# A two-layer graph-attention kernel: first steps with W1's loads and sums elsewhere and one scaling inside a sum; last group in another order, with its last norms applied on VectorE

## Chip, cores and metric

One core of a Trainium2 chip. The metric is the device time of one execution in microseconds (us), lower is better. The engines are TensorE (PE; PEld is its weight load), VectorE (DVE), ScalarE (ACT), GpSimd (POOL), and SyncE (SP), whose queue issues nearly all transfers here.

## What is computed

The input x holds 128 graphs of 128 nodes with 512 features in float32, adj holds a 128 x 128 adjacency matrix for each. Cut to what matters:

```python
# layer 0, 8 heads of 64
q, k, v = x @ Wq + bq, x @ Wk + bk, x @ Wv + bv
logits  = where(adj > 0, q k^T / sqrt(64), -1e9)          # per head
out     = softmax(logits) v                               # heads side by side
x       = layernorm(x + relu(out @ Wo + bo))
# layer 1, one head
Wh      = x @ W
e       = leaky((Wh @ a1)[:, None] + (Wh @ a2)[None, :])  # slope 0.2
att     = softmax(where(adj > 0, e, -9e15), over the first index)
x       = layernorm(x + leaky(att @ Wh))
```

## The kernel before

**Matrix products by seven.** Every product with a weight matrix is done by a Strassen scheme (Winograd's form): 7 block products in place of 8. The weight's side needs four block sums, made once (`right_blocks`, L149 to L156): t2 = t2 - t0, t5 = t3 - t2, t4 = t5 - t0, t6 = t1 - t5. The left side needs four sums for each group of graphs (`left_blocks`, L269 to L280, on GpSimd). The pieces of one product are named p1 to p7 (the block products on TensorE), t0, t2, t3 (copies of a bank by ScalarE between products that go into the same bank), and c11, c12, c21, c22 (result blocks, mostly by VectorE). p1 uses weight block 0, p5 block 2 (t2), p6 block 5, p2 block 1, p7 block 4, p4 block 6, p3 block 3 (`PLACE`, L147). p7 goes into p6's bank after t2 has been copied.

**Loop.** Graphs go in groups of 4. Q, K and V are made for a group at once (L366 matmuls, 128 x 256 results); pairs of graphs share the product with Wo (layer 0) and with W1 (layer 1) (L447). The loop runs over steps t = -3 to 123 (L974), one graph a step: scores (L518), mask and maxima on VectorE (L532, L541), exponentials and divisions on ScalarE (L552, L566), a store of the attention weights to DRAM (L573) and a fetch that re-reads them in blocks (L579), from which VectorE transposes (L583, paT), and a step later the product with V (L596, p_oT). `group()` takes the next step of the next group's Q, K and V, `pair()` the next of a pair's. V's weight blocks are kept in DRAM and fetched one by one into a ring of three buffers (wv_n, L407).

**First steps.** Wq's blocks 0 and 1 are scaled by 1/8 (L944), the first products start, and `other_half` (L959) takes graphs 2 and 3, then block 2: scaled, minus block 0; then `add_x`, the four left sums on GpSimd; then block 3: scaled, and the other three sums, on VectorE. In step 0 the loads of W1 are made into chores (L1006): two broadcasts of the vector a (256 KB each) and eight of W1 (128 KB each), of which each `group()` issues two. W1 gets an extra column W1 a: 8 `dots` of two VectorE instructions each (L205), four `last_column` of two (L220), then the four block sums; `w1_chores(4)` takes four of these 16, twice in step 3 (all dots) and twice in step 5.

**Order.** All five engines' queues have the order in which the code issues them (`manual_schedule`, L874): an engine takes its instructions in order, and a waiting one holds what is behind it.

**Last group.** The last four graphs' layer 0 and the last eleven graphs' layer 1 are written as one list, `PLAN` (L1231), of pieces name.method: v is the last group's V; s0 to s3 its softmaxes; sl, el, al what the loop left; a0 to a2 pairs of layer 0 (by, bw preload a bank with the bias); b0 to b4 pairs of layer 1; e0 to e10 the attention of layer 1 of graphs 117 to 127, x, m loads. An e runs sender (L794, ACT), turn (L798, PE transpose), add (ACT), maxima (DVE), exp (ACT), divide (DVE), product (L837, PE), copy (ACT), residual (L847, L848, DVE), stats (DVE), rstd (L646, L648, POOL), apply, store. With `on_scalar` (L649 to L660) rstd makes two more small GpSimd results (L651, L653), and the apply is a ScalarE instruction (L657); without it the apply is on VectorE (L661).

```python
1223    for n in range(11):
1224        jobs[f"e{n}"] = Edge(
...
1227            on_scalar=True,
```

Of the kernel before, what the change touches and what calls it, by code (L numbers as in the profile page):

```python
# [12 lines left out]
ALU = mybir.AluOpType  # L13
# [11 lines left out]
def kernel(  # L25
# [59 lines left out]
    nc = tc.nc  # L85
# [5 lines left out]
    QSCALE = 1.0 / float(HD) ** 0.5  # L91
# [54 lines left out]

    PLACE = (0, 1, 3, 6, 2, 5, 4)  # L147

    def right_blocks(t):  # L149

        return [
            lambda: nc.vector.tensor_sub(t[2], t[2], t[0]),
            lambda: nc.vector.tensor_sub(t[5], t[3], t[2]),
            lambda: nc.vector.tensor_sub(t[4], t[5], t[0]),
            lambda: nc.vector.tensor_sub(t[6], t[1], t[5]),
        ]  # L156

    def places(w):
        return [w[:, n] for n in range(7)]
# [30 lines left out]
    def load_w1():  # L190
# [7 lines left out]
        loads = [load_a(0), load_a(1)] + block_loads(W1, columns(w1), nc.sync)  # L198
# [30 lines left out]
        ops = [dots(k, o, c) for k, o in every for c in range(2)]  # L229
        return loads, ops + [last_column(k, o) for k, o in every] + right_blocks(places(w1))  # L230

    X, XT, XS, Q, K, V, MF, OT, X1T, X1, WH = ({} for _ in range(11))

# [662 lines left out]
    chores = []  # L896
# [46 lines left out]
    def scale(n):  # L943
        nc.vector.tensor_scalar_mul(wq[:, n], wq[:, n], QSCALE)  # L944

    wq_sums = right_blocks(places(wq))
    turned = [order_features(b) for b in range(2)]
    keep_busy(14)
# [10 lines left out]
    def other_half():  # L959

        for b in (2, 3):
            transpose_rows(b, order_features(b), nc.scalar.copy)
        scale(2)
        wq_sums[0]()
        add_x()
        scale(3)
        for op in wq_sums[1:]:
            op()

    chores += right_blocks(places(wk)) + load_wv()  # L970
    END = B - GROUP
# [2 lines left out]
    for t in range(-3, END):  # L974
# [17 lines left out]
        def w1_chores(n):  # L992
            for op in [w1_sums.pop(0) for _ in range(n)]:
                op()
# [7 lines left out]
        if t == 0:  # L1002
            load_blocks(Wo, columns(wo), nc.sync, spread_rows=False)
            late_chores = right_blocks(places(wo)) + load_bias()
            w1_loads, w1_sums = load_w1()
            chores += w1_loads  # L1006
        if t == 1:
            chores += late_chores

# [32 lines left out]
        elif t == 4:  # L1042
# [14 lines left out]
            layer.store(0)  # L1057
            layer.fetch(1)
            layer.fetch(0)
            sm.exp(6, 7)  # L1060
            group()
            sm.reciprocals(0)
# [3 lines left out]
        else:  # L1066
            sm.maxima()
            group()
            if t == 3:
                w1_chores(4)  # L1070
            if t == 5:
                turn_x1(4)
                x1_sums()
# [11 lines left out]
            pair()  # L1085
            sm.exp(0, 1, 2, 3)
            edge.exp()
            if t in (3, 5):
                w1_chores(4)
            pair()  # L1090
            sm.exp(4, 5)
            last.transpose()
# [130 lines left out]
    for n in range(11):  # L1223
        jobs[f"e{n}"] = Edge(
            END - 7 + n,
            {"z": z_homes[n % 4], "e": part(wk, 6, n % 4), "att": part(wk, 5, n % 4)},
            on_scalar=True,
        )
    for n in range(6):
        jobs[f"x{n}"] = jobs[f"m{n - 2}"] = Load(END - 2 + n)  # L1230
    PLAN = """  # L1231
        v.p5 x0.x el.residual m1.adj s0.scores m2.adj v.fetch al.apply.0 x1.x b0.p1
        sl.transpose al.fetch.1 v.p6 b0.t0 s0.add.0 m1.cast s0.add.1 m3.adj al.store.0
        s1.scores s0.reduce v.t2 v.fetch v.p2 m1.mask s0.exp.4.5 s1.add.0 s1.add.1 s0.exp.6.7
        al.fetch.0 s1.reduce b0.p6 s0.exp.0.1 b0.p5 s0.exp.2.3 v.c11 v.fetch s1.exp.4.5 v.p7
        s0.reciprocals.1 s0.reciprocals.0 el.stats s0.divide.2.3 al.transpose.1 s0.divide.4.5
        el.rstd b0.p2 b0.t2 al.transpose.0 s0.divide.0.1 b0.p7 al.sum.0 b0.c11 s0.divide.6.7
        b1.p1 al.sum.1 s1.exp.6.7 s0.store al.sum.2 b0.t3 s1.reciprocals.1 s1.exp.0.1 b0.p4
        b0.c22 al.sum.3 s1.divide.4.5 b0.p3 b0.c21 s0.fetch s1.divide.6.7 s2.scores b0.c12 v.t3
        e0.sender e0.turn s1.exp.2.3 v.c22 v.p4 m2.cast s1.reciprocals.0 e0.add m2.mask s2.add.0  # L1240
        s1.divide.2.3 v.p3 s2.add.1 s1.divide.0.1 b1.t0 s2.reduce s1.store v.c21 b1.p6 el.apply
        v.c12 s2.exp.2.3 el.store s3.scores e0.maxima s2.exp.6.7 s1.fetch sl.attend e0.exp
        s2.exp.4.5 e0.divide e1.sender e1.turn b1.p5 s0.transpose sl.copy e0.product m3.cast
        s2.reciprocals.1 sl.sum.0 e1.add m3.mask b1.p2 s3.add.0 s2.divide.6.7 sl.sum.1
        s1.transpose s2.divide.4.5 a0.by a0.p1 sl.sum.2 b1.t2 e0.copy sl.sum.3 b1.p7 b1.c11 a0.t0
        s3.add.1 s2.exp.0.1 a0.p6 s3.reduce b1.t3 s0.attend a0.t2 e0.residual s3.exp.0.1 a0.p7
        s3.exp.6.7 a0.bw a0.p5 b1.c22 x2.x a0.t3 s2.reciprocals.0 e1.maxima s3.exp.2.3 a0.p4
        s2.divide.0.1 a0.c22 b1.p3 e1.exp s3.reciprocals.0 s2.divide.2.3 a0.c21 a0.p3 e1.divide
        s3.divide.0.1 s2.store a0.stats.1 e1.product s3.divide.2.3 b1.c12 a0.rstd.1 s3.exp.4.5
        s1.attend e0.stats e1.copy e3.sender e3.turn s3.reciprocals.1 e0.rstd b1.p4 s0.copy e1.residual  # L1250
        s2.fetch s1.copy a0.p2 e1.stats x3.x s3.divide.6.7 a0.c11 s1.sum.0 a0.c12 s3.divide.4.5
        s1.sum.1 e3.add s3.store a0.stats.0 s1.sum.2 e0.apply a1.by a1.p1 b1.c21 e1.rstd e0.store
        e3.maxima a0.apply.1 e2.sender e2.turn a1.p2 a1.t0 a0.store.1 s2.transpose e3.exp a0.rstd.0 a1.p6
        e2.add s3.fetch e1.apply e2.maxima a1.bw a1.p5 s1.sum.3 a1.t2 a0.apply.0 e3.divide a1.p7
        e1.store e2.exp a1.c11 a0.fetch.1 s2.attend e2.divide a1.t3 a1.c22 a1.p4 s2.copy
        a0.store.0 s3.transpose a1.p3 a1.c21 a1.stats.1 s3.attend a0.transpose.1 a0.fetch.0
        a1.rstd.1 e3.product s3.copy a1.c12 e2.product e3.copy a1.stats.0 s3.sum.0 a2.p2
        a1.apply.1 s3.sum.1 e3.residual e2.copy a1.store.1 a2.bw a2.p5 s3.sum.2 a0.transpose.0 a2.by a2.p1
        a1.rstd.0 x5.x e2.residual b2.p1 a2.t0 a0.sum.0 a1.apply.0 a1.fetch.1 a2.p6 a2.c11
        s3.sum.3 b2.t0 e2.stats b2.p5 a0.sum.1 a2.t2 e3.stats x4.x a0.sum.2 a2.p7 a1.store.0  # L1260
        a0.sum.3 b2.p6 a2.t3 e2.rstd a2.c22 a2.p4 b2.t2 a1.transpose.1 a2.p3 e3.rstd e2.apply
        a1.fetch.0 a2.c21 b2.p7 a2.stats.1 e3.apply e4.sender e4.turn a2.c12 a2.rstd.1 b2.p2 e2.store
        b2.t3 e3.store e4.add b2.p4 a2.stats.0 a2.apply.1 b2.c22 a2.rstd.0 b2.c21 a2.store.1
        b2.c11 b2.p3 a1.transpose.0 e6.sender e6.turn e4.maxima a2.apply.0 a1.sum.0 b3.p1 e6.add
        a2.store.0 a1.sum.1 b2.c12 b3.p2 e4.exp e6.maxima b3.t0 a2.fetch.1 a1.sum.2 e5.sender e5.turn
        b3.p6 e4.divide a1.sum.3 e5.add e6.exp e5.maxima e4.product b3.t2 a2.fetch.0 e6.divide
        e5.exp b3.p7 b3.c11 e4.copy e5.divide e6.product b3.t3 e4.residual b3.p5 e6.copy
        e4.stats e5.product a2.transpose.0 e4.rstd b3.p4 e5.copy a2.transpose.1 b4.p2 b3.c22
        b3.c21 a2.sum.0 e4.apply e6.residual b4.p1 a2.sum.1 e4.store b3.p3 a2.sum.2 b4.t0
        e6.stats a2.sum.3 b4.p6 b3.c12 e6.rstd b4.c11 b4.p5 b4.t2 e5.residual b4.p7 e6.apply  # L1270
        e5.stats e8.sender e8.turn e6.store e7.sender e7.turn b4.t3 e8.add b4.p4 b4.c22 e5.rstd e7.add e8.maxima
# [50 lines left out]
```

## Time and profile before

| | us |
|---|---|
| median of 3 runs | 2402.37 (2400.96 to 2404.64) |
| the profiled execution | 2402.25 |
| its span, first to last instruction | 2400.4 |
| mean granted TensorE clock | 0.995 of full |
| PE busy | 2363.4 (98%) |
| PE waits listed, 0 to 100 us | 12.9 |
| PE waits listed, 175 to 2300 us | 1.2 |
| PE waits listed, 2300 to 2401 us | 11.8 |

The span is the time between the first and the last instruction of one execution. The list of waits names the engine and line that stood idle and what released it; a wait for several semaphores is put down to the one that came last by the profile, which can be the wrong one. A row of the timeline has start, duration, engine, line, operation, result and operands, shape, count, and in brackets the idle time before it. The table of stretches has, for each, the busy time and the clock that TensorE was granted, as a part of full speed.

### The profile page before, as it was taken

The page shows a single profiled execution, that of the slowest core. Times are in us where ns is not written, and L with a number is a line of the kernel's source. Part 1 is how long each engine was busy: PE and PEld are TensorE (multiplying, and loading weights), DVE is VectorE, ACT ScalarE, POOL GpSimd, SP SyncE. Part 2 cuts the span into 40 slices and gives each one's busy share as a digit, 9 for nine tenths or more (in the row PEclk, how much of TensorE's full clock was granted, in tenths as well). Part 3 has the DMA queues.
Part 4 walks back from the last instruction along what each step waited for, and adds up shares of the span by engine and source line. Part 5 has one row for each costly group of instructions (what it writes and reads, how often), then busy time and mean ns, then how long its engine had stood idle before and what let it go on. Part 6 is the DMA issues. An engine that isn't in the chain of part 4 may idle for free.

```text
span 2400.4 us, 44153 instructions
## 1 busy us (share of the span) xinstructions
PE 2363.4 (98%) x13362; PEld 1980.3 (82%) x13362; DVE 1827.0 (76%) x3719; ACT 1517.3 (63%) x5463; POOL 811.1 (34%) x1195
## 2 busy tenths in 40 slices
PE   8999999999999999999999999999999999999996
PEld 7888888888888888888888888888888888888874
DVE  5677787777777877877777778778778777777777
ACT  3666666566666666665666666666666666666685
POOL 1232333233333333332333433333323334333335
PEclk9999999999999999999999999999999999999999
DMA  7455555555546545555545555555554554554452
GB/s 205 158 165 160 174 163 162 176 161 158 179 147 186 164 154 174 160 165 181 159 154 183 154 176 167 156 173 157 169 181 157 157 179 155 173 175 151 156 170 98
DMA packets 435566, 395.32 MB, mean 165 GB/s; under 512 B 108280, under 2 KB 339328, under 8 KB 435328
## 3 DMA queue, kind: packets, MB, share of 16 engines
q1 hardware_dynamic: 435008, 392.23, 52.3%
q8 instruction: 107, 1.75, 0.3%
q14 instruction: 131, 1.07, 0.1%
q10 hardware_dynamic: 320, 0.26, 0.0%
HBM read 248.58 MB, written 143.72 MB: 163 GB/s over the span
## 4 chain that ended last, share of the span: by engine, by line
PE 91%; DVE 3%; DMA 2%; ACT 2%; issue 1%; SPq 1%; POOL 1%; DVEq 0%; ACTq 0%; POOLq 0%
PE st_y L366 27%; PE p_y L447 17%; PE st_w L366 13%; PE p_w L447 9%; PE st_x L366 7%; PE lg L518 6%; PE p_oT L596 5%; PE p_x L447 4%; PE p_h L837 4%; DMA wv_n<-wv 1%; ACT pa L552 0%; DMA x_dram<-x 0%; DMA wq<-in_L_gnn_Wq_dram 0%; ACT pa L566 0%; POOL rstd L648 0%
## 5 line engine op out<-in xcount | busy, mean ns | idle before, releaser
L552 ACT ACTIVATE pa<-pa,nmax 128x128 f32<-128x128 f32 x1008 | 392.6, 393 | 5.9 <-DVE nmax L541 5.5
L646 POOL TENSOR_SCALAR ve<-mv 128x1 f32<-128x1 f32 x256 | 69.9, 273 | 855.9 <-DVE mv L642 847.1
L566 ACT ACTIVATE pa<-pa,rs 128x128 f32<-128x128 f32 x1008 | 334.1, 395 | 8.6 <-DVE rs L562 8.5
L275 POOL TENSOR_TENSOR oS<-oT 128x256 f32<-128x256 f32 x63 | 45.8, 727 | 643.4 <-ACT oT L610 643.4
L532 DVE TENSOR_TENSOR pa<-lg,mf 128x512 f32<-128x512 f32 x252 | 161.9, 684 | 99.9 <-PE lg L518 99.6
L458 ACT COPY pr_t<-p_y 128x257 f32<-128x257 f32 (+1 forms) x375 | 137.7, 367 | 135.7 <-PE p_y L447 133.3
L343 ACT COPY st_t<-st_y 128x512 f32<-128x512 f32 x192 | 110.5, 575 | 144.2 <-PE st_y L366 143.1
L552 ACT ACTIVATION_READ_ACCUMULATOR pa<-pa,nmax 128x1 f32 x1008 | 192.3, 191 | 0.0
L347 ACT ACTIVATE st_t<-st_y,b_cols 128x256 f32<-128x256 f32 x192 | 80.6, 471 | 164.9 <-PE st_y L366 164.9
L648 POOL TENSOR_TENSOR rstd<-ve,mhalf 128x1 f32<-128x1 f32 x256 | 177.0, 691 | 21.4
L596 PEld LDWEIGHTS p_oT<-paT,v 128*64 128x64 f32 x2016 | 107.5, 136 | 91.8 <-PE st_y L366 44.0
L610 ACT ACTIVATE oT<-p_oT,b_cols 128x128 f32<-128x128 f32 x504 | 144.2, 368 | 60.0 <-PE p_oT L596 58.9
L583 DVE STREAM_TRANSPOSE paT<-paz 128x1024 f32<-128x1024 f32 x126 | 156.9, 1245 | 3.3 <-DMA paz<-pa_dram 2.1
L541 DVE TENSOR_REDUCE nmax<-pa 128x8 f32<-128x1024 f32 x126 | 153.7, 1220 | 4.4
L518 PE MATMUL lg<-kT,qT 64*128 64x128 f32 x2048 | 148.7, 285 | 0.0
L518 PEld LDWEIGHTS lg<-kT,qT 64*128 64x128 f32 x2048 | 124.2, 187 | 22.9 <-issue 22.9
L596 PE MATMUL p_oT<-paT,v 128*64 128x128 f32 x2016 | 137.9, 279 | 0.3 <-DVE paT L583 0.3
L768 DVE TENSOR_TENSOR wh<-p_w,pr_t 128x257 f32<-128x257 f32 x122 | 51.9, 425 | 104.0 <-PE p_w L447 64.1
L447 PE MATMUL p_y<-wo,oT 128*128 128x256 f32 x504 | 129.9, 380 | 0.7 <-ACT pr_t L458 0.6
L447 PE MATMUL p_y<-wo,oS 128*128 128x256 f32 x504 | 129.4, 379 | 0.0
L447 PE MATMUL p_y<-w,x1T 128*128 128x257 f32 x496 | 128.2, 381 | 0.2 <-DVE x1T L245 0.2
L447 PE MATMUL p_y<-w,x1S 128*128 128x257 f32 x496 | 128.0, 380 | 0.0
(201 smaller groups left out, 6032.8 us busy)
## 6 DMA issues: line engine op xcount, KB each, us to landing
pa_dram<-pa SPq DMA_DIRECT2D x126, 512.0 KB, 3.0
paz<-pa_dram SPq DMA_DIRECT2D x504, 128.0 KB, 2.8
wv_n<-wv SPq DMA_DIRECT2D x224, 256.0 KB, 2.8
x<-in_x_dram SPq DMA_DIRECT2D x128, 256.0 KB, 2.9
x_dram<-x SPq DMA_DIRECT2D x128, 256.0 KB, 2.5
xz<-x_dram SPq DMA_DIRECT2D x512, 64.0 KB, 2.0
xz<-in_x_dram SPq DMA_DIRECT2D x496, 64.0 KB, 2.2
out_dram<-z SPq DMA_DIRECT2D x120, 256.0 KB, 2.3
```

The costliest lines, as they stand in the source:

```text
L366: nc.tensor.matmul(p[:, m, :], lhs, rhs, start=start and m == 0 and kc == 0, stop=True, skip_group_check=True,)
L447: nc.tensor.matmul(p[:, :width], xs()[n][:, kc, :], w[:, PLACE[n], kc, :], start=start and kc == 0, stop=True, skip_group_check=True,)
L458: nc.scalar.copy(t[:, :width], p[:, :width])
L518: nc.tensor.matmul(self.lg[r][:, c, :], q[rows, c, cols], k[rows, c, cols], start=c == 0, stop=True, skip_group_check=True,)
L532: nc.vector.tensor_add(by_head[:, r * NC : (r + 1) * NC], self.lg[r].rearrange("p c (b k) -> p c b k", b=4), mf.unsqueeze(1).to_broadcast( ...
L541: nc.vector.tensor_reduce(self.nmax, by_head, AX.XY, ALU.max, negate=True)
L552: nc.scalar.activation(self.pa[:, :, h, :], self.pa[:, :, h, :], AF.Exp, bias=self.nmax[:, h : h + 1], accum_out=self.sums[:, h : h + 1],)
L566: nc.scalar.activation(self.pa[:, :, h, :], self.pa[:, :, h, :], AF.Copy, scale=self.rs[:, h : h + 1])
L583: nc.vector.transpose(self.paT.rearrange("p h (a i) -> p a h i", i=32), self.paz.rearrange("p a (h k) -> p a h k", k=32),)
L596: nc.tensor.matmul(self.oT[r * HD : (r + 1) * HD, c, :], v[:, h * HD : (h + 1) * HD], self.paT[:, r * NC + c, :], start=c == 0, stop=True, ...
L610: nc.scalar.activation(OT[pair][:, c, h * P : (h + 1) * P], self.oT[:, c, :], AF.Identity, bias=b_cols[:, 1, c : c + 1],)
L648: nc.gpsimd.tensor_tensor(self.r, ve, mhalf, ALU.pow)
```

## The change

Five edits. The scaling of Wq's blocks 2 and 3 goes into their sums (`scaled_less`, one instruction each); block 3 itself is scaled after the sums. W1's loads leave the chores: four are issued in each of steps 0, 1 and (two) 2, between the store and the fetch of the attention weights. The dots are taken 3 and 2 in step 3 and 3 in step 4, the last columns in step 5 after the divisions. W1's block sums go to GpSimd, after the last columns. In the last group the list has the same 445 pieces in another order, and e7 to e10 have their norms applied on VectorE.

```diff
-    def right_blocks(t):
+    def right_blocks(t, engine=nc.vector):
         return [
-            lambda: nc.vector.tensor_sub(t[2], t[2], t[0]),
+            lambda: engine.tensor_sub(t[2], t[2], t[0]),
...
-        return loads, ops + [last_column(k, o) for k, o in every] + right_blocks(places(w1))
+        ops += [last_column(k, o) for k, o in every]
+        return loads, ops, right_blocks(places(w1), nc.gpsimd)
...
+    def scaled_less(n, left, right):
+
+        nc.vector.scalar_tensor_tensor(
+            wq[:, n], wq[:, left], QSCALE, wq[:, right], op0=ALU.mult, op1=ALU.subtract
+        )
...
-        scale(2)
-        wq_sums[0]()
+        scaled_less(2, 2, 0)
         add_x()
+        scaled_less(5, 3, 2)
+        for op in wq_sums[2:]:
+            op()
         scale(3)
-        for op in wq_sums[1:]:
-            op()
...
-            w1_loads, w1_sums = load_w1()
-            chores += w1_loads
+            w1_loads, w1_sums, w1_blocks = load_w1()
...
             layer.fetch(0)
+            w1_chores(3)
             sm.exp(6, 7)
...
             if t == 3:
-                w1_chores(4)
+                w1_chores(3)
...
-            if t in (3, 5):
-                w1_chores(4)
             pair()
...
             coming.store_sender()
+            if t in (3, 5):
+                w1_chores(2 if t == 3 else 4)
             if t == 5:
-                w1_chores(4)
+                for op in w1_blocks:
+                    op()
...
         sm.store()
+        if 0 <= t < 3:
+            for load in w1_loads[4 * t : 4 * t + 4]:
+                load()
...
-            on_scalar=True,
+            on_scalar=n < 7,
...
-        v.p5 x0.x el.residual m1.adj s0.scores m2.adj v.fetch al.apply.0 x1.x b0.p1
...
-        a1.fetch.0 a2.c21 b2.p7 a2.stats.1 e3.apply e4.sender e4.turn a2.c12 a2.rstd.1 b2.p2 e2.store
...
-        b4.p3 b4.c21 e7.maxima e8.exp e10.sender e10.turn e5.apply b4.c12 e7.exp e5.store e8.divide
-        e9.sender e9.turn e10.add e7.divide e8.product e9.add e10.maxima e7.product e8.copy e9.maxima
-        e10.exp e7.copy e8.residual e9.exp e8.stats e10.divide e8.rstd e9.divide e10.product
-        e7.residual e9.product e8.apply e10.copy e8.store e7.stats e9.copy e10.residual e7.rstd
-        e10.stats e7.apply e9.residual e7.store e10.rstd e9.stats e10.apply e10.store e9.rstd
-        e9.apply e9.store
+        el.residual v.p6 x0.x m2.adj m1.adj al.apply.0 x1.x e0.sender sl.transpose s0.scores
...
+        a0.transpose.1 e4.sender e3.turn s3.copy a1.p5 b1.c12 e1.stats a0.fetch.0 a1.t2 s3.sum.0
...
+        b3.c22 b4.p1 a2.sum.0 e6.copy e5.stats e8.add a2.sum.1 e7.turn b3.p3 b4.t0 e8.maxima
+        e5.rstd e6.residual e8.exp b4.p2 b4.p6 a2.sum.2 e5.apply e8.divide b3.c12 e8.product
+        a2.sum.3 b4.t2 e6.stats e5.store e7.add b4.p7 b4.c11 e8.copy e6.rstd e7.maxima e9.sender
+        b4.p5 e8.residual b4.t3 e7.exp e9.turn b4.p4 e6.apply e7.divide e6.store b4.c21 e8.stats
+        e7.product e10.sender b4.c22 e8.rstd e10.turn e7.copy b4.p3 e10.add e7.residual
+        e10.maxima b4.c12 e10.exp e8.apply e9.add e10.divide e8.store e9.maxima e10.product
+        e7.stats e9.exp e10.copy e9.divide e7.rstd e10.residual e9.product e9.copy e10.stats
+        e9.residual e10.rstd e9.stats e10.apply e9.rstd e7.apply e10.store e7.store e9.apply
+        e9.store
```

More of the change, by code (lines that the diff above doesn't have):

```diff
@@ L147 @@
     PLACE = (0, 1, 3, 6, 2, 5, 4)
-    def right_blocks(t):
+    def right_blocks(t, engine=nc.vector):
         return [
[L152 to L155, printed above, removed]
+            lambda: engine.tensor_sub(t[2], t[2], t[0]),
+            lambda: engine.tensor_sub(t[5], t[3], t[2]),
+            lambda: engine.tensor_sub(t[4], t[5], t[0]),
+            lambda: engine.tensor_sub(t[6], t[1], t[5]),
         ]
@@ L1231 @@
     PLAN = """
-        v.p5 x0.x el.residual m1.adj s0.scores m2.adj v.fetch al.apply.0 x1.x b0.p1
[L1233 to L1260, printed above, removed]
@@ L1261 @@
-        a0.sum.3 b2.p6 a2.t3 e2.rstd a2.c22 a2.p4 b2.t2 a1.transpose.1 a2.p3 e3.rstd e2.apply
-        a1.fetch.0 a2.c21 b2.p7 a2.stats.1 e3.apply e4.sender e4.turn a2.c12 a2.rstd.1 b2.p2 e2.store
[L1263 to L1271, printed above, removed]
-        b4.p3 b4.c21 e7.maxima e8.exp e10.sender e10.turn e5.apply b4.c12 e7.exp e5.store e8.divide
@@ new lines @@
+        al.store.0 v.t2 al.fetch.1 v.p5 el.stats m2.cast s0.add.0 m1.cast el.rstd m3.adj s0.add.1
+        s1.scores al.fetch.0 s0.reduce el.apply b0.p1 m2.mask s0.exp.4.5 el.store m1.mask
+        s2.scores s1.add.0 v.fetch s0.exp.6.7 v.fetch s1.add.1 b0.p2 s0.exp.2.3 s1.reduce
+        sl.attend s0.exp.0.1 al.transpose.0 v.p2 s1.exp.6.7 al.transpose.1 s1.exp.2.3
+        s0.reciprocals.0 al.sum.0 s0.reciprocals.1 s0.divide.0.1 v.p7 al.sum.1 v.c11 v.fetch
+        s0.divide.6.7 al.sum.2 s0.divide.2.3 al.sum.3 b1.p1 s0.divide.4.5 v.t3 s0.store b0.t0
@@ new lines @@
+        v.p4 v.c22 s1.exp.0.1 b0.c11 s1.exp.4.5 s1.reciprocals.0 v.p3 s1.divide.0.1 s2.add.0
+        s0.fetch s1.divide.2.3 s2.add.1 v.c21 s2.reduce b0.p6 e1.sender m3.cast b1.p5 sl.copy
+        m3.mask v.c12 s1.reciprocals.1 s2.exp.0.1 b1.p2 sl.sum.0 s0.transpose b0.t2 sl.sum.1
+        s1.divide.4.5 b0.p7 sl.sum.2 s1.divide.6.7 sl.sum.3 s2.exp.6.7 s1.store s2.exp.2.3 b0.t3
+        s2.reciprocals.0 s2.exp.4.5 b0.p4 s2.divide.0.1 s1.fetch s2.reciprocals.1 b0.c21
+        s2.divide.6.7 s3.scores a0.by a0.bw a0.p1 s2.divide.4.5 s3.add.0 b1.t0 a0.p5 s3.add.1
@@ new lines @@
+        a0.t0 e2.sender s3.reduce e1.turn b0.p5 s2.divide.2.3 s2.store a0.p6 s1.transpose
+        s3.exp.6.7 a0.p2 s3.exp.0.1 b0.c22 a0.t2 b1.p6 a0.c11 s3.exp.4.5 a0.p7 s2.fetch b1.t2
+        s3.reciprocals.1 s3.exp.2.3 b1.p7 a0.t3 s3.reciprocals.0 b0.p3 s3.divide.6.7 a0.c22
+        s3.divide.0.1 a0.p4 b0.c12 s3.divide.2.3 a0.p3 e1.add a0.c21 s3.divide.4.5 a0.stats.1
+        e2.turn b1.t3 s3.store e1.maxima e2.add a0.rstd.1 b1.p4 e2.maxima e1.exp a0.c12 e2.exp
+        a0.apply.1 e1.divide e0.turn s3.fetch s0.attend a0.stats.0 e0.add e0.maxima e1.product
@@ new lines @@
+        a0.rstd.0 s0.copy s2.transpose a0.store.1 s1.attend e0.exp e2.divide e1.copy s2.attend
+        e0.divide s1.copy e1.residual e0.product a0.fetch.1 a1.by s1.sum.0 a1.p2 s2.copy
+        s3.transpose s1.sum.1 a1.p1 e0.copy x3.x s1.sum.2 b1.c11 s3.attend a0.apply.0 b1.c22
+        s1.sum.3 e0.residual e3.sender a0.store.0 b1.p3 a1.t0 a1.bw a1.p6 a1.c11 b1.c21 x2.x
+        a0.transpose.1 e4.sender e3.turn s3.copy a1.p5 b1.c12 e1.stats a0.fetch.0 a1.t2 s3.sum.0
+        e0.stats e3.add a1.p7 s3.sum.1 e3.maxima s3.sum.2 a1.t3 e3.exp a1.p4 a1.c22 s3.sum.3
@@ new lines @@
+        e3.divide a1.p3 e1.rstd a1.c21 a1.stats.1 a2.by a2.bw e3.product e0.rstd a1.c12 e1.apply
+        a2.p5 e3.copy e1.store a2.p1 a1.stats.0 a1.rstd.1 e0.apply e2.product e3.residual a2.t0
+        e0.store a2.p6 a1.rstd.0 a1.apply.1 e3.stats x5.x a2.p2 e2.copy a1.store.1 a0.transpose.0
+        a2.t2 e3.rstd a1.apply.0 a2.p7 e2.residual a1.store.0 b2.p1 a0.sum.0 a2.t3 e2.stats
+        e3.apply x4.x a0.sum.1 b2.p2 a1.fetch.1 a2.c22 b2.t0 e2.rstd a2.p4 b2.c11 a2.p3 a2.c11
+        e5.sender e3.store a2.c21 a0.sum.2 e2.apply a1.fetch.0 b2.p6 a2.stats.1 a0.sum.3 e4.turn
@@ new lines @@
+        a2.c12 b2.p5 a2.rstd.1 b2.t2 e4.add e2.store b2.p7 e4.maxima a2.stats.0 e4.exp e5.turn
+        b2.t3 e4.divide a2.apply.1 a2.rstd.0 b2.p4 b2.c22 a1.transpose.0 a2.store.1 b2.p3 b2.c21
+        a1.transpose.1 e6.sender b3.p1 a2.apply.0 b2.c12 a1.sum.0 e6.turn e5.add e4.product
+        a2.store.0 a1.sum.1 b3.t0 e5.maxima a2.fetch.1 e6.add a1.sum.2 b3.p5 e5.exp e6.maxima
+        e4.copy a1.sum.3 b3.p6 e5.divide e6.exp e4.residual e5.product a2.fetch.0 b3.t2 b3.p7
+        e4.stats e5.copy b3.p2 e5.residual e4.rstd b3.t3 b3.p4 b3.c11 e4.apply e6.divide
@@ new lines @@
+        a2.transpose.1 e6.product b3.c21 e4.store a2.transpose.0 e8.sender e7.sender e8.turn
+        b3.c22 b4.p1 a2.sum.0 e6.copy e5.stats e8.add a2.sum.1 e7.turn b3.p3 b4.t0 e8.maxima
[3 more added lines that the diff above has]
+        e7.product e10.sender b4.c22 e8.rstd e10.turn e7.copy b4.p3 e10.add e7.residual
```

## The prediction

> **What bounds the kernel now.** I read the page's busy shares first, then the matmul engine's (PE's) waits over the whole span, then its waits and rows in the first 100 us and in the last 110 us.
>
> ```profile
> span 2400.4 us, 44153 instructions
> PE 2363.4 (98%) x13362; PEld 1980.3 (82%) x13362; DVE 1827.0 (76%) x3719; ACT 1517.3 (63%) x5463; POOL 811.1 (34%) x1195
> ```
>
> PE is busy in all but 37.0 us. Its waits list shows only 1.2 us between 175 and 2300 us, so nothing in the body can be gained unless PE's own work shrinks, and the change leaves the number and shapes of the matmuls as they are. What can move lies at the two ends. The waits of the first 100 us, in the order line, releaser, total, times, longest:
>
> ```profile
> PE st_w L366 <- DVE kT L384: 2.8, 1, 2.8
> PE st_w L366 <- DMA wv_n<-wv: 2.8, 1, 2.8
> PE st_w L366 <- DMA wk<-in_L_gnn_Wk_dram: 2.6, 1, 2.6
> ```
>
> The releaser of the third is put down wrongly: that product reads wq and xS, and the wq sum (L152) ends at 15.02, just ahead of it (rows below). After each of these waits the clock falls. Columns of the stretches: length, busy time of PE, PEld, DVE, ACT, POOL, granted clock, DMA share, GB/s:
>
> ```profile
> 56.00:60.00 4.00, 3.96 (x12) 3.29 (x13) 1.25 (x2) 1.15 (x6) 0.00 (x0) 0.65 0.27 102
> 94.00:98.00 4.00, 3.74 (x10) 2.95 (x11) 1.64 (x7) 3.38 (x11) 0.00 (x0) 0.59 0.00 0
> 16.00:20.00 4.00, 3.58 (x11) 2.41 (x10) 3.93 (x6) 0.00 (x0) 1.47 (x2) 0.57 1.04 255
> ```
>
> So a wait of 2.6 to 2.8 us costs itself and about 1.75 us of slow matmuls after it; waits of 2.4 and 2.1 us (at 2335 and 2359) were followed by a clock of 1.00. [...]
>
> All sums below are made against the profiled execution: 2402.25 us, 1.85 us of it outside the span; the median of the runs, 2402.37, is 0.12 above it.
>
> **Part 1, one scaling inside a sum (Wq).** VectorE, then GpSimd beside it:
>
> ```profile
> 12.03 1.33 DVE L944 TENSOR_SCALAR wq<-wq 128x512 f32<-128x512 f32 x1 [2.26 <-DMA wq<-in_L_gnn_Wq_dram]
> 13.39 1.63 DVE L152 TENSOR_TENSOR wq<-wq 128x512 f32<-128x512 f32 x1
> 14.95 1.48 DVE L944 TENSOR_SCALAR wq<-wq 128x512 f32<-128x512 f32 x1
> 16.46 1.63 DVE L153 TENSOR_TENSOR wq<-wq 128x512 f32<-128x512 f32 x1
> ```
>
> ```profile
> 11.81 1.26 POOL L275 TENSOR_TENSOR xS<-xT 128x512 f32<-128x512 f32 x1 [10.52 <-ACT xT L941]
> 13.15 1.32 POOL L276 TENSOR_TENSOR xS<-xS,xT 128x512 f32<-128x512 f32 x1
> 14.44 1.71 POOL L277 TENSOR_TENSOR xS<-xT 128x512 f32<-128x512 f32 x1
> ```
>
> Each VectorE step ends 0.3 us (scaling) or 0.55 us (sum) after the GpSimd step beside it (13.36 after 13.07, 15.02 after 14.47). The change makes one fused step of the first pair and one of the second. No fused step of this size stands beside a GpSimd step of this size in the trace: bounds are 0.69 us (L847, same form, alone) and 1.63 us (L152 here); I take the pattern of the sums, since it too reads two tensors. Then wq's block 2 is ready at 13.07 + 0.55 = 13.62 and block 5 at 14.47 + 0.55 = 15.02, in place of 15.02 and 18.09. Product p5 starts at 13.7 in place of 15.12, behind 1.2 us of idleness and so with no slow clock; p6 at 13.7 + 1.73 = 15.45 in place of 18.24. Before p7 ScalarE still has to copy p6's bank (0.84 us behind p6's end at 17.35), so p7 starts at 18.3 in place of 21.86: **-3.5 us** (-4.1 with fused steps of 0.69; -3.5 with 1.63; 0 if two GpSimd steps pass per fused step). What is late next: Wk was in use by VectorE at 19.94 without a wait, p1 of Wk would need it at 20.1; the first V block was issued at 28.52 and lands 2.4 to 3.0 us later, and is needed at 35.75 - 3.5 = 32.2.
>
> **Part 2, W1's loads.** They were spread through step 0 on SP's queue: two of 256 KB and two of 128 KB stand ahead of the seventh V block's fetch (48.20), four more behind it. That fetch landed 7.7 us after its issue (page median 2.8). Landing after 3 us it is there at 51.2, and its product starts when p4 lets it, at 51.27 + 1.72 = 52.99, not 56.05: 3.06 us. The two products from 56.05 to 61.26 took 5.21 for 3.45 of full-clock slots: 1.76 us. Together **-4.8 us**. The loads now go behind the store of the attention weights, into SP's wait for its landing (L573 at 53.17 to L579 at 58.72), so they cost the queue nothing; but the re-reading fetch stands behind them in the transfers: 0.77, 0.51 and 0.26 MB in steps 0, 1, 2, up to 3.1, 2.1 and 1.0 us at the 245 GB/s of 54 to 56 us. Step 0, with PE 8.3 us earlier: p_oT wants paT at 59.9; the fetch is issued near 52.1, the last part lands at 56.6 to 59.7, the transpose takes 1.25: 57.9 to 61.0. So PE waits 0 to 1.1 us there; I charge **+0.5**.
>
> **Part 3, W1's row sums.** Sixteen steps (L205, one each 0.465 us) hold VectorE from 84.83 to 92.46, ahead of paT and of the kT sum that PE waits for:
>
> ```profile
> 94.26 3.38 PE L366 MATMUL st_w<-xT,wk 128*128 128x256 f32 x8 [2.83 <-DVE kT L384]
> ```
>
> Six stay; the kT sum comes 10 x 0.465 = 4.65 us sooner, more than the 2.83 waited. From 94.26 to 99.50 PE took 5.24 us for 3.46 of slots: 1.78 more. **-4.6 us.** Four go behind the reciprocals, where VectorE next waited 2.33 us for ScalarE (L693, 97.01): they fit (1.9). Six (2.8 us) go between the v sums at 108.92 and 111.27, where 1.65 was idle: the second ends at 113.1, its bank is wanted at 114.49. The last columns follow the reciprocals of step 5, and the four block sums leave VectorE (2.7 us, in a stretch where it is 98% busy) for GpSimd, idle there from 124.0 to 132.39. At 1.27 to 1.71 each (L275, L277) they take 5.1 to 6.8 us, to 132.0 to 133.7; the first product that reads one starts at 136.70. I put this at 0 (-0.6, the 0.63 wait at 128.23, to +0.5). [...]
>
> **Part 4, the last group.** PE's work is the same, in another order. From 2292.41 to the last pair's first product at 2371.47 PE waited 5.6 us: 2.39 at 2335 for ScalarE (busy 9.1 to 10 of each 10 us from 2300 to 2340), 2.11 at 2359 for a sender behind two norms, the rest small. Adding slots (1.73, 0.87, 1.09, 1.03, 0.2 us by kind) the new order has 69.07 us ahead of that product, the old 69.73: -0.7. ScalarE's work ahead of PE's runs up to 3.1 us over PE's in the new order, 3.2 in the old, so the 2335 kind of wait stays; e4's sender now stands well ahead of its turn, so the 2.11 goes, and I give back half for new ones: -1.0 (bounds -5.6, no waits, to +5.6, twice as many). The tail: the old end is p4's end (2379.54) plus 20.9 us.
>
> ```profile
> 2387.25 2.62 PE L837 MATMUL p_h<-wh,wk 128*128 128x512 f32 x4 [3.02 <-DVE wk L832]
> 2396.62 0.81 ACT L657 ACTIVATE wq<-wq,shift,rstd 128x512 f32<-128x512 f32 x1 [0.74 <-POOL shift L653]
> ```
>
> In the new order e8's product and e9's turn already lie ahead of p4, and behind it VectorE has one nearly unbroken chain: bank sums 0.86, maxima 1.16, divides 0.92, residuals 4.2, statistics 2.6, four applies 2.1 (0.53 each, L661): 11.9 us, 1.0 until it starts, 0.7 to 1.5 of short waits for e10's and e9's exponentials. The last rstd (0.8 without minus and shift) lies beside two applies. With 3.0 from apply to the end, 16.6 to 17.4: **-3.9 us**. Part 4: -0.7 - 1.0 - 3.9 = **-5.6**.
>
> Sum: -3.5 - 4.8 + 0.5 - 4.6 - 5.6 = -18.0; 2402.25 - 18.0 = **2384 us**.
>
> **Rivals.** (a) The loads only change place: the fetches of steps 0 to 2 land late, p_oT waits, and a wait over 2.6 us drags the clock: 3.1 + 1.75 in step 0, 2.1 in step 1, so parts 2 and 3 lose 7: 2391. For it: DMA is at 1.1 around every burst; against: 1 to 3 us of slack. (b) The new order also loses ScalarE's 2335 wait and the small ones: 4.6 more, 2379. For it: ScalarE is busy only 4.6 of the 10 us before 2300; against: the equal sums. (c) The fused scaling does nothing, because the products wait for GpSimd's xS: 2387.7; against: xS is there at 13.07 and 14.47. (d) Slower: turns stand apart from their senders and PE takes its queue in order, so a turn whose sender is late holds everything. A wait of 2.6 with the slow clock costs 4.4; to lose the 17 of the rest and 4.8 more, 5 of the 11 turns must do so; six give 2402.25 - 17.0 + 26.4 = 2412. Against: the longest such wait now is 2.1 (five in all, 4.8 us), and a turn set later waits less.
>
> **Numbers.** 0.2% is 4.8 us, about what a measurement can tell from no change. Forecast (2380 to 2389, with (c)) 0.58; (b) 0.15; (a) 0.17; gains eaten to within 0.2% 0.06; (d) 0.04. So faster 0.90, same 0.06, slower 0.04. The range 2376 to 2395 leaves out less than half of (b) and (a)'s upper part.
>
> **What would show it.** p7 of Wq at 18.3; no wait on wv_n or on kT in the first 100 us and no clock under 0.9 there after 20 us; p_oT of step 0 near 60; the last group's first product 12 us earlier; p4 to end 17 us. Wrong if a wait above 2.6 us stands anywhere new in the first 140 us, or if p_e waits add up to more than 8 us.

## The result and the profile after

| | before | after | forecast |
|---|---|---|---|
| median, us (range) | 2402.89 (2400.96 to 2405.53) | 2393.45 (2391.58 to 2393.51) | 2384 (2376 to 2395) |
| ratio, 95% interval | | 0.9953 [0.9941, 0.9965] | |
| profiled execution, us | 2402.25 | 2393.51 | |
| its span, us | 2400.4 | 2391.6 | |
| mean granted clock | 0.995 | 0.998 | |
| PE waits listed, 0 to 100 us | 12.6 | 7.6 | |

The direction is right and the time lies in the range, but the profiled executions differ by 8.7 us where 18 were summed. A fifth execution of after, at a granted clock of 0.556, took 4113.27 us; the range is that of the other four, whose median is 2393.18. The ratio with its interval comes with each measurement and is not the quotient of the two medians in the table. (The sums of the waits of 0 to 100 us are added up from the rows; the 12.9 in the table further up is 0.3 too high.)

In what follows a run's **lead** at some moment is the start of a matmul in the profile of before less the start of the same matmul in that run; TensorE's order is the same in both up to the last group. It was worked out from the two traces, and it tells in which stretch time was won or lost:

| lead on before, us, at | 50 us | 65 | 91 | 104 | 180 | 2291 | the end |
|---|---|---|---|---|---|---|---|
| forecast | 3.5 | 8.3 | 7.8 | 12.4 | 12.4 | 12.4 | 18.0 |
| after | 1.0 | 6.0 | 5.1 | 9.9 | 9.9 | 4.6 | 8.8 |

So 2.5 us are missing at 50 us, the next steps gain what was summed, 5.2 us go lost between 180 and 2291 us, and the last group gives 4.1 instead of 5.6.

The page of after, its span and its engines:

```profile
span 2391.6 us, 44137 instructions
PE 2360.3 (99%) x13362; PEld 1976.1 (83%) x13362; DVE 1825.5 (76%) x3718; ACT 1515.4 (63%) x5459; POOL 814.6 (34%) x1191
```

PE's waits of the first 100 us in after (line, releaser, total, times, longest):

```profile
PE st_w L367 <- DVE qT L385: 1.8, 1, 1.8
...
PE st_w L367 <- DVE wq L949: 1.2, 1, 1.2
PE p_oT L597 <- DVE paT L584: 1.0, 2, 0.8
```

The three waits of 2.6 to 2.8 us are gone. The one on wq is 1.2 now. A new one leads the list, for c22, the sum that makes a block of qT, which the prediction did not look at. Stretches of after that answer to those shown of before (length, busy time of PE, PEld, DVE, ACT, POOL, granted clock, DMA share, GB/s):

```profile
51.00:55.00 4.00, 4.00 (x20) 3.54 (x19) 3.51 (x6) 1.68 (x7) 0.00 (x0) 1.00 0.53 185
86.00:90.00 4.00, 4.00 (x20) 3.53 (x19) 3.28 (x11) 1.96 (x7) 0.00 (x0) 1.00 0.32 131
```

Where before had clocks of 0.65 and 0.59, the same work now runs at 1.00. The tail of after, PE and then VectorE:

```profile
2373.86 1.03 PE L448 MATMUL p_y<-w,x1T 128*128 128x257 f32 x4
...
2379.77 1.15 PE L838 MATMUL p_h<-wh,wk 128*128 128x512 f32 x2 [2.62 <-DVE wk L833]
```

```profile
2385.73 0.69 DVE L641 BATCH_NORM_STATS2 st<-wq 128x6 f32<-128x512 f32 x1
2386.46 0.18 DVE L643 BATCH_NORM_AGGREGATE mv<-st 128x2 f32<-128x6 f32 x1
2386.56 0.97 DVE L662 TENSOR_SCALAR wq<-wq,mv,rstd 128x512 f32<-128x512 f32 x2
2387.98 0.55 DVE L662 TENSOR_SCALAR wq<-wq,mv,rstd 128x512 f32<-128x512 f32 x1 [0.45 <-POOL rstd L649]
```

From the end of b4's p4 (2374.85, the start of the next product) to the end of the span are 16.8 us, before 20.9. VectorE is nearly unbroken, and the last rstd costs it 0.45.

### The profile page after: what moved, and what is told of

It is laid out like the page before. It is cut to its first block, busy times and chain, and to the rows that moved or that the text cites. A ratio compares the mean times of both kernels' runs of the same rounds, so it can differ in the third digit from the quotient of the medians.

```text
span 2391.6 us, 44137 instructions
## 1 busy us (share of the span) xinstructions
PE 2360.3 (99%) x13362; PEld 1976.1 (83%) x13362; DVE 1825.5 (76%) x3718; ACT 1515.4 (63%) x5459; POOL 814.6 (34%) x1191
## 3 DMA queue, kind: packets, MB, share of 16 engines
q8 instruction: 107, 1.75, 0.3%
## 4 chain that ended last, share of the span: by engine, by line
PE 84%; DVE 4%; DMA 4%; ACT 4%; SPq 2%; issue 2%; POOL 1%; DVEq 0%; POOLq 0%; ACTq 0%
PE st_y L367 24%; PE p_y L448 16%; PE st_w L367 12%; PE p_w L448 8%; PE st_x L367 6%; PE lg L519 5%; PE p_oT L597 5%; PE p_h L838 4%; PE p_x L448 4%; ACT pa L567 1%; DMA x_dram<-x 1%; ACT pa L553 1%; SPq L241 1%; DVE st L641 1%; DMA e_dram<-e 1%
```

## The experiments

Theory A: the three parts work as summed, but Part 1 runs into the new wait, and the body loses time to transfers that land late by chance. Its rivals: the body's loss is a consequence of the lead, or belongs to the new order of the loads. e1 to e4, e5 to e8 and e9 to e12 ran side by side with the kernel before, which took 2403.03, 2403.13 and 2402.57 us (medians). Each of these three occasions was on another chip (15, 14 and 0); for the first measurement of after the chip is not on record.

| run | median, us (range) | ratio to before, 95% interval |
|---|---|---|
| e1, scaling only | 2402.26 (2397.49 to 2404.83) | 0.9991 [0.9982, 1.0] |
| e2, W1's work only | 2395.72 (2392.68 to 2396.19) | 0.9966 [0.9953, 0.9978] |
| e3, last group only | 2398.47 (2395.21 to 2400.64) | 0.9979 [0.997, 0.9988] |
| e4, after, c22 first | 2387.88 (2386.23 to 2388.74) | 0.9935 [0.9922, 0.9947] |
| e5, after again | 2388.64 (2387.13 to 2391.01) | 0.9943 [0.9931, 0.9955] |
| e6, after, Wv ahead of x1 | 2386.47 (2385.46 to 2386.86) | 0.9932 [0.992, 0.9944] |
| e7, after, norms on ScalarE | 2390.33 (2389.0 to 2396.88) | 0.9953 [0.994, 0.9966] |
| e8, after, block sums on VectorE | 2390.34 (2388.3 to 2391.29) | 0.9948 [0.9936, 0.996] |
| e9, e4 and e6 together | 2386.0 (2384.69 to 2386.76) | 0.9929 [0.9916, 0.9941] |
| e10, before, Wv ahead of x1 | 2400.57 (2397.39 to 2402.85) | 0.9987 [0.9978, 0.9995] |
| e11, W1's loads only | 2399.77 (2396.43 to 2401.03) | 0.9987 [0.9978, 0.9996] |
| e12, transposes in the waits | 2407.33 (2403.7 to 2413.03) | 1.0017 [1.0008, 1.0026] |

Their leads on the profile of before:

| lead, us, at | 50 us | 65 | 91 | 104 | 180 | 2291 | the end |
|---|---|---|---|---|---|---|---|
| e1 | 1.0 | 2.1 | 2.1 | 2.1 | 1.4 | -0.5 | -1.3 |
| e2 | 0.6 | 5.3 | 5.2 | 10.0 | 8.9 | 8.0 | 6.5 |
| e3 | -0.2 | 2.2 | 2.2 | 2.5 | 2.5 | 0.1 | 1.9 |
| e4 | 3.1 | 8.0 | 7.7 | 12.4 | 12.3 | 11.6 | 15.6 |
| e5 | 0.5 | 6.1 | 5.8 | 10.6 | 11.0 | 11.4 | 15.1 |
| e6 | 1.3 | 6.0 | 5.5 | 10.3 | 10.6 | 11.7 | 15.8 |
| e7 | 1.3 | 6.0 | 6.0 | 10.8 | 10.3 | 9.4 | 11.6 |
| e8 | 0.8 | 5.9 | 4.7 | 9.4 | 9.8 | 8.4 | 10.9 |
| e9 | 3.2 | 7.9 | 7.5 | 12.3 | 11.4 | 12.5 | 16.2 |
| e10 | 0.1 | 0.3 | 0.3 | 0.3 | 1.5 | 2.6 | 1.2 |
| e11 | -0.1 | 4.6 | 4.6 | 5.2 | 5.4 | 4.0 | 4.1 |
| e12 | -3.1 | -0.7 | -0.7 | -0.7 | -0.6 | -9.7 | -10.7 |

**e1: before with the scaling alone** (scaled_less as in the change).

```
-        scale(2)
-        wq_sums[0]()
+        scaled_less(2, 2, 0)
         add_x()
-        scale(3)
-        for op in wq_sums[1:]:
+        scaled_less(5, 3, 2)
+        for op in wq_sums[2:]:
             op()
+        scale(3)
```

> The kernel before with the scaling-in-a-sum part alone. Both theories: p7 of Wq's group near 18.5 us instead of 21.9 (the trace of after has 18.53). Theory A (the term of 3.5 us was mis-sized, because Q's sum c22, which frees the bank for p3, stands on VectorE behind the eight block sums of Wk and Wv): p3 starts after a wait of 1.8 us, the lead at p1 of the second group is 1.3 us, and the time is 1.3 us less, with a scatter of 2 us from the body. Rival B (the summed 3.5 us arrive, and the wait in after comes only with the other parts): no wait at p3, lead 3.3 us, time 3 us less.

p7 started at 18.52, and p3 then waited 1.83 us for c22: A.

```profile
25.77 1.97 PE L366 MATMUL st_w<-xT,wq 128*128 128x256 f32 x8 [1.83 <-DVE qT L384]
```

The lead is 1.0 us at 50 us. The half clock behind V's p3 came here too, at 54.9 us. What the time keeps, 0.8 us, its interval does not tell from nothing.

**e2: before with W1's loads, dots and block sums moved** (after without the lines of e1 and with the old last group).

> The kernel before with W1's loads, dots and block sums in their new places, and the rest as before. The lead on before at 180 us should be 8.6 us (9.86 in after, less 1.27 that the scaling gave). Theory A (the body's stalls are transfers that land late by chance, whatever the lead is): 8.6 us less in time, with a scatter of 3 us either way, and the stalls of the body at other places than in after. Rival B (the lead itself is given back in the body, since queues run closer to their transfers): the lead shrinks by about 5 us between 140 and 2290 us, at the same places as in after (390, 538, 612, 1473, 1932 us), and the time is 3.5 us less.

The lead was 8.9 us at 180 us and still 8.0 at 2291: in this execution the lead was not given back, which speaks against rival B. The time is 7.3 us less. The lead of 0.6 us at 50 us does not come from the edit: here the first wait of 2.63 us, which e2 shares with before, was not followed by a half clock.

**e3: before with the new last group** (the new list and `on_scalar=n < 7`).

> The kernel before with the new order of the last group and the last four norms on VectorE, and the rest as before. Theory A: the stretch from the loop's last attention product to the end takes 104.8 us instead of 109.0 (as in after), and the time is 4.2 us less (2 us of scatter from the body). Rival B (the order was fitted to what stands ahead of it and needs the other parts): the stretch takes 107 us or more, time 2 us less or none.

4.6 us less (by the ratio 5.0, 2.9 to 7.2), which is A's time and not B's. The profiled execution shows only 1.8 us from 2291 to the end (the stretch takes 107.2 us, B's figure), with a half clock at 2317 that after does not have; without its 1.75, the cost of a half clock in the start of before, that would be 3.6. So the new order gains without the other parts, though this one trace shows less than the medians.

**e4: after with c22 ahead of Wv's sums.**

```
-            for _ in range(min((3 if t == -3 else 2 if t >= 0 else 1) * n, len(chores))):
+            for _ in range(min((first_chores.pop(0) if t == -3 else 2 * n if t >= 0 else n), len(chores))):
...
+    first_chores = [2, 1, 1, 11]
```

> The kernel after, with the four block sums of Wv emitted behind Q's sum c22 on VectorE instead of ahead of it. Theory A (p3 of Q waits 1.8 us for c22, which stands behind eight block sums): the wait goes, p3 starts 1.8 us earlier, and the time is 1.8 us less than after, 2391.6 us (2 us of scatter from the body). Rival B (what is late next takes it: Wv's blocks are summed and written later, so that the fetch for the first product of V lands behind its due time): a wait of 1 us or more on wv_n at V's first product, and the time within 0.8 us of after.

In after c22 stands in VectorE's queue behind eight sums, in e4 behind four. VectorE and PE in after:

```profile
22.29 0.68 DVE L152 TENSOR_TENSOR wv_t<-wv_t 128x512 f32<-128x512 f32 x1
...
24.94 0.68 DVE L385 TENSOR_TENSOR qT<-st_w,st_t 128x512 f32<-128x512 f32 x1
```

```profile
25.77 1.96 PE L367 MATMUL st_w<-xT,wq 128*128 128x256 f32 x8 [1.82 <-DVE qT L385]
```

and in e4:

```profile
22.27 0.68 DVE L385 TENSOR_TENSOR qT<-st_w,st_t 128x512 f32<-128x512 f32 x1
22.88 0.68 DVE L152 TENSOR_TENSOR wv_t<-wv_t 128x512 f32<-128x512 f32 x1
```

```profile
23.77 1.89 PE L367 MATMUL st_w<-xT,wq 128*128 128x256 f32 x8
```

c22 comes 2.67 us earlier, p3 starts 2.0 us earlier without a wait, V's first product has none either, and the lead at 50 us is 3.1 us. The cause of 2.1 of the missing 2.5 us is shown. From there on the trace follows the sum: the lead is 12.4 us at 104 us, as forecast. The median is 5.6 us under that of after, more than the edit explains; e5 tells why. Against e5's median of 2388.64 it is 0.8 us less, and the intervals overlap, so that the edit's 2 us stand in the traces alone.

**e5: after, unchanged.**

> The kernel after, unchanged, for a second profile of its body. Theory A (the 5.3 us that it lost on before between 140 and 2290 us are transfers that happened to land late, of Wv's blocks above all): the lead on before at 180 us is again 9.9 us, the body's loss is another one, at other places, between 0 and 4 us, and the median lies at 2390.3 us (2403.0 less the 12.7 that the three parts gave alone). Rival B (the body's loss belongs to this kernel): the lead shrinks at 390, 538, 612, 1473 and 1932 us as before, and the median is 2393.5 us again.

The same program took 2388.64, 4.8 us less than on the first occasion, with before at 2402.89 there and 2403.13 here. The start is much the first one's (lead 10.6 at 104 us, 9.9 there); of the body's loss nothing came back: the lead grew from 11.0 to 11.4. Rival B is out. PE's listed waits from 175 to 2200 us, after first:

```profile
PE st_y L367 <- DMA wv_n<-wv: 2.7, 4, 1.1
PE p_y L448 <- ACT pr_t L459: 1.4, 3, 0.7
```

and e5:

```profile
PE st_y L367 <- DMA wv_n<-wv: 0.3, 1, 0.3
```

At six waits that after has in the body and before has not, the lead falls by 0.1 to 0.3 us more than the row shows, as the matmuls start again (at 538 us the wait is 1.09; the lead falls by 1.26 at that matmul and by 0.10 at the next).

**e6: after with Wv's load ahead of x1's.**

```
             self.apply(0)
             self.store(0)
-            self.fetch(1)
-            self.fetch(0)
+            gone.append(self)
...
             sm.maxima()
             group()
+            if gone:
+                layer = gone.pop()
+                layer.fetch(1)
+                layer.fetch(0)
```

> The kernel after, with the eight loads that bring x1 back from DRAM emitted behind the first group step of the loop's body instead of ahead of it, so that on SyncE's queue the load of a block of Wv goes ahead of them. Theory A (PE's waits on wv_n in the body come from that load's standing behind loads that wait for the landing of x1's stores; the margin is about zero, so that each late landing costs): the listed waits on wv_n between 175 and 2200 us, 2.7 us in after and 1.2 to 2.0 in four other looks, fall under 0.5 us, and the time is 1.5 to 2.5 us under the unchanged kernel of the same call. Rival B (what is late next takes it: x1's loads come later and the products of layer one wait, or the blocks of Wv land no earlier): waits of the same sum or more, no gain.

SyncE's queue in after, at the longest of the waits:

```profile
526.01 0.34 SPq L713 DMA_DIRECT2D x_dram<-x  x1
...
528.63 6.43 SPq L241 DMA_DIRECT2D xz<-x_dram  x8
535.16 0.39 SPq L408 DMA_DIRECT2D wv_n<-wv  x1
```

and PE there:

```profile
537.83 1.35 PE L367 MATMUL st_y<-wv_n,xS 128*128 128x256 f32 x5 [1.09 <-DMA wv_n<-wv]
```

The block of Wv could be fetched once p5 had freed its buffer, at 528.9, but eight loads stand ahead of it that wait for x1's stores to land. It is issued at 535.16, 2.67 us ahead of the product that reads it. The same place in e6:

```profile
527.18 0.32 SPq L408 DMA_DIRECT2D wv_n<-wv  x1
527.60 4.20 SPq L241 DMA_DIRECT2D xz<-x_dram  x8
```

Here it is issued as soon as p5 ends. The list from 175 to 2200 us has no row left, the median is 2.2 us under e5's, and the range is 1.4 us wide instead of 3.9. The intervals of the two ratios overlap, but the slowest of the five executions here (2386.86) is under the fastest of e5's five (2387.13). A holds.

**e7: after with the last norms back on ScalarE** (`on_scalar=True`).

> The kernel after, with the norms of the last four batches applied on ScalarE as before, in the new order. Theory A (the tail's last chain is GpSimd's rstd, then the apply; on ScalarE it has two more sums of GpSimd, 0.23 and 0.19 us with 0.08 between, and an apply of 0.81 instead of 0.55): the last store is issued 0.8 us later, time 0.8 us more; up to 1.5 if the three last norms queue on ScalarE. Rival B (VectorE is the tail's bound, and each apply taken from it brings the last statistics forward by 0.5 us): time equal or up to 1 us less.

1.7 us above e5 in the median, with intervals that overlap. In the traces e7 is 2.6 us behind e5 at 2296 us, nearly all of it in waits on wv_n, and loses another 0.9 from there to the end. The tail's 0.9 is close to A's 0.8.

**e8: after with W1's block sums on VectorE** (`right_blocks(places(w1), nc.vector)`).

> The kernel after, with W1's four block sums on VectorE instead of GpSimd, at the same place in the order. Theory A (VectorE is late in steps 5 and 6, since W1's dots stand there: PE's waits at layer one's first products in after, 0.4 us in all and 1.5 in the run with W1's part alone, are its lateness passed on by the maxima and ScalarE): four more sums of 0.7 us make them 1.5 to 2.8 us longer, and the time 1.5 us more. Rival B (VectorE has room there, and the move to GpSimd gave nothing): no difference.

At layer one's first products nothing waits (0.25 us at 135 us in e5). Between 104 and 180 us, where the sums stand, e8 and e5 gain 0.3 us each on before. The medians differ by 1.7 us, with intervals that overlap. The profiled executions differ by 4.2: 1.2 at a wait for paT at 63 us, ahead of the moved sums, 1.8 in the body, with four waits on wv_n, and most of the rest at a half clock at 2309 that e5 does not have. Rival B: the move to GpSimd gave nothing that can be seen. The eight small sums of the last columns (L220) take VectorE 1.72 us in after, where the last of them, beside the first of GpSimd's sums (L152, 1.29 us), took 1.26 and the other seven 0.13 to 0.15 each; in e8 the eight take 0.61. PE shows no gain or loss from it.

**e9: e4's and e6's edits together.**

> The kernel after with both edits: Q's sum c22 ahead of Wv's block sums, and Wv's loads ahead of x1's. Theory A (the two waits stand at different places and add): no wait of PE at p3 of Q, no listed wait on wv_n from 175 to 2200 us, and 1.8 us less than the run with the second edit alone, so some 2384.7 us (before at 2403.1). Rival B (one takes the other's gain, since an earlier PE meets V's first blocks before they have landed): 2386.5 us, as with the second edit alone.

Both waits are gone, and the lead is 3.2 us at 50 us. At 117 us PE waited 1.69 us for ScalarE's copy of a bank, and 1.2 us of the lead went there. So in the trace they add in part. The median of 2386.0 is the lowest of all kernels here, but 0.5 us under e6 is a difference that the intervals do not tell from nothing.

**e10: before with e6's edit.**

> The kernel before, with Wv's loads ahead of x1's in the body and nothing else changed. Theory A (the chance part of the body is in both kernels alike, 1.2 to 2.4 us of waits on wv_n per run): no listed wait on wv_n between 175 and 2200 us, the time 1.5 to 2.5 us under before, and the runs closer together. Rival B (only the changed kernel runs into it): no difference.

No wait on wv_n, the lead grows by 1.1 us in the body, the time is 2.0 us less (by the ratio 3.1, 1.2 to 5.3). That the runs lie closer together is not shown (11 over 5.5 us, 27 of before over 7.6). So before has such waits too, and loses them by the same edit.

**e11: before with W1's loads moved and nothing else.**

```
-            chores += w1_loads
...
         sm.store()
+        if 0 <= t < 3:
+            for load in w1_loads[4 * t : 4 * t + 4]:
+                load()
```

> The kernel before with W1's twelve loads in their new place and nothing else changed; its dots and block sums stay. Theory A (the loads held back the last block of Wv's first use): the wait of 2.8 us at 56 us goes with the half clock behind it, the wait on kT at 94 us stays, the lead at 90 us is 4.5 to 5 us, time 4.7 us less. Rival B (the loads alone do nothing, since the sums stand in VectorE's queue as before, and what is late next takes the wait): the lead at 90 us under 1.5 us, time 1 us less.

The wait at 56 us goes with its half clock, lead 4.6 us at 65 us; the 2.82 on kT stays. The time is only 2.8 us less, where A had 4.7; in the trace the body took 1.4 back, in waits on wv_n. The mechanism is A's. (There are ten loads: four, four and two.)

**e12: before with transposes in the two waits.** They read the identity and write a bank that nobody reads.

```
+        if g < 2:
+            late = chains[2 - g][6]
+            chains[2 - g][6] = lambda: (keep_busy(8), late())
```

> The kernel before with eight transposes of the identity, whose result nobody reads, put on TensorE ahead of p3 of V in the first group and p3 of K in the second, so that they run in the waits at 56 and 94 us. Theory A (the clock is judged in windows of 3.41 us at a fixed beat: of the windows seen so far, those in which PE idled 0.6 or more were followed by a half clock, those under 0.5 by none, and a half clock costs 1.75 us): the two waits end as late as before, less than 0.1 us after the old ends, but no clock under 0.9 follows them, and the time is 3.5 us less. Rival B (the half clock follows the time since the last product that counts, or the transposes delay the products): no gain, or a loss of up to 1 us.

At the first wait A holds: no half clock, and e12 makes up 2.4 us on before between 50 and 65 us, 0.8 of it because PE, late by 3.1 us, came to the load later and waited less. At the second it fails: the eight transposes took 0.9 us, PE still idled 1.95, and the half clock came (stretches of e12):

```profile
91.71:95.12 3.41, 1.46 (x11) 1.13 (x10) 3.31 (x12) 0.07 (x1) 0.00 (x0) 1.00 0.00 0
95.12:98.53 3.41, 3.41 (x9) 2.69 (x9) 1.05 (x4) 3.31 (x11) 0.00 (x0) 0.50 0.00 0
```

And the kernel is 4.8 us slower in the median, which neither theory expected. In the profiled execution, the slowest of the eleven, 2.9 us went from 16 to 26 us, where the half clock lasted 10.24 us instead of 3.41 after the same wait of 2.63. 9.0 went in the body: eleven waits on wv_n (5.7 us listed, and their restarts) and one for a copy. In this execution the stores of the attention weights took 4.18 us (median) to land in one of their three DRAM tiles and 2.96 and 3.05 in the others; the loads behind them on SyncE's queue come later by as much. Why that tile is slow there stays open, as does whether the transposes have a part in it.

## Why the prediction was right in direction and half the size

- **The range.** The forecast's middle was missed by 9 us. The time lies inside because the range left room for rival (a), whose waits did not come in that size. That the losses which nobody had summed stayed within that room was luck.
- **Part 1, -3.5: the step that failed.** The scaling gave what was worked out as far as p7 (18.53, forecast 18.3; p6's start, 13.7 + 1.73, is 15.43 and not 15.45, which changes nothing). The prediction then asked what is late next, and looked at Wk and at V's blocks, not at the bank that p3 writes: its reader c22 stood behind eight sums on VectorE. Measured: -1.0 at 50 us. e1 shows the wait with this part alone, e4 that it goes when c22 stands ahead of four of the sums. What the part is worth also changes with the half clock behind the old start: with the old scaling the lead at 50 us was 0.6 where none came (e2), -0.2 to 0.1 where it lasted 3.41 us (e3, e10, e11) and -3.1 where it lasted 10.24 (e12).
- **Part 2, -4.8 + 0.5.** Measured between 50 and 65 us: -5.0, and then 0.84 lost, mostly in the wait on paT (0.77). e11: -4.7 from the loads alone. Rival (a) is out.
- **Part 3, -4.6.** Measured between 91 and 104 us: -4.8; GpSimd's block sums at 0 are borne out by e8.
- **"Nothing in the body can be gained": the second step that failed.** The 1.2 us of waits in one profile were read as a property of the kernel. In the profiles without e6's edit the lead from 180 to 2291 us moved by +0.4 (e5) to -5.2 us (after) and -9.0 (e12), and the listed waits on wv_n add up to anything from none (e2) to 5.7 us (e12). e6, e9 and e10 show that these waits go with the place of one load in a queue, which leaves PE's work as it is. In after they make up 2.7 us of waiting; 1.4 are waits for ScalarE's copies, nearly all at 1473 to 1476 us, after VectorE had waited 4.99 us at 1465 for a batch's edge terms from DRAM; the restart adds 0.1 to 0.3 at six of the seven waits, and the seventh (0.91 at 612 us) before has as well, with 0.54 at 619. Why an occasion is bad throughout, as the first was for after (all four between 2391.6 and 2393.5, all five of e5 between 2387.1 and 2391.0), stays open; the occasions differ in the chip, and no run tests that.
- **Part 4, -5.6.** The tail is right: 20.9 became 16.8, -4.1 for -3.9. The waits ahead of it are not: -1.0 was charged, but the rows add up to 6.4 us in after where those of before add up to 5.7, so that the 0.7 of less work went too. From the loop's last attention product to the last pair's first product it takes 80.2 us, before 80.1. The wait on a sender (2.1) did go; copies of banks on ScalarE and two products behind a divide took its place. So rival (b), by which the waits for ScalarE go, is out. The main rows of after, 2287 to 2367 us:

```profile
PE p_y L448 <- ACT wk L459: 2.6, 3, 1.8
PE p_h L838 <- DVE wk L833: 1.3, 2, 0.8
PE p_y L448 <- ACT pr_t L459: 1.0, 2, 0.5
```

- **Rival (c)**, scaling without effect, was wrong at p7 and near the truth by p3, for a reason that it didn't name. **(d)**: p_e waits 0.8 us in all of the last group, before 4.8. No new wait over 2.6 us stands in the first 140 us.

Profile against profile the sum reads -1.0 - 5.0 + 0.8 - 4.8 at the start, +5.3 up to 2291 us, -4.1 in the last group: -8.8. On the second occasion (e5) it is -10.6, -0.8 and -3.7: -15.1. The ratios of the two occasions are 0.9953 and 0.9943, with intervals that overlap: some 11 to 14 us less, where 18 were forecast.

## What to carry to other kernels

When a stall goes, follow every buffer and bank that the next products write, and look for its reader in the in-order queue of its engine; a reader behind work that is not urgent can be the next stall, as c22 behind eight sums was here (a wait of 1.82 us in after, none in e4, where it stands behind four). In after the eight loads that wait for x1's stores took 6.43 us of SyncE's queue at 528.63, and the block of Wv behind them was issued at 535.16, in e6, ahead of them, at 527.18: so put the load with a fixed due time ahead of the one that must wait anyway. A profile is one execution: the listed waits on wv_n came to 2.7 us in after and to 0.3 in e5, which is the same program, so look at the margin of the transfers, not at the list of waits alone.

## What the runs showed of the hardware

The length of a wait alone does not decide the clock, as waits of 1.97 us in e3 and 1.96 in e1 show below. In each execution with more than one half clock, each of these starts at a whole number of 3.413 us from every other, and lasts one such stretch or several. In before the first three start at 16.20, 57.16 and 94.71 us, 12 and 11 times 3.413 apart, and each of them lasts 3.413; the one of 10.24 in e12 is three. The beat differs from execution to execution: the half clock behind V's p3 starts at 57.16 in before and at 54.91 in e1. So I divided each of the fourteen traces into such windows and worked out PE's idle share of each, up to some 2365 us. Of the windows that PE idled 0.40 to 0.50 of, none of 13 was followed by a half clock; of those at 0.53 to 0.59, five of 14; of those at 0.62 or more, all of 12. What decides between 0.53 and 0.59 stays open. The wait at 56 us in before fell within one window, here with the one after it:

```profile
53.75:57.16 3.41, 1.11 (x5) 1.04 (x6) 1.68 (x2) 1.79 (x9) 0.00 (x0) 1.00 0.98 251
57.16:60.57 3.41, 3.41 (x9) 2.71 (x9) 1.78 (x3) 0.00 (x0) 0.00 (x0) 0.50 0.24 83
```

A wait of 1.97 us at the same product in e3 ended in the middle of a window, which idled 0.42 and was followed by a clock of 1.00:

```profile
54.04:57.45 3.41, 1.96 (x9) 1.79 (x10) 1.64 (x2) 1.75 (x9) 0.00 (x0) 1.00 0.72 220
57.45:60.86 3.41, 3.41 (x18) 3.00 (x17) 3.30 (x7) 1.64 (x7) 0.00 (x0) 1.00 0.43 129
```

One of 1.96 us in e1 filled 0.57 of its window and was followed by 0.50. So the prediction's line between waits of 2.4 and 2.6 us was an accident of the beat: the 2.39 us at 2335 in before fell across two windows (0.31 and 0.44), and a wait of 1.8 us can be followed by a half clock in one execution and not in the next. The same wait of the last group, in windows that idled 0.53 both times, in after and then in e3, where the matmuls behind it ran at half clock:

```profile
2311.70 1.14 PE L448 MATMUL p_y<-w,x1T 128*128 128x257 f32 x4 [1.82 <-ACT wk L459]
```

```profile
2316.78 1.83 PE L447 MATMUL p_y<-w,x1T 128*128 128x257 f32 x4 [1.82 <-ACT wk L458]
```
